# Two layers in one kernel: the second layer's first norm moved behind the first layer's last diagonal, and the norm's square moved from ACT to DVE

## The chip, the cores and the metric

The kernel runs on one core of a Trainium2 chip. Times are microseconds (us) on the device, from the program's first to its last instruction; the time of a kernel is the median of several runs. Engines are named as the profile names them: PE (TensorE matmuls), PEld (its weight loads), DVE (VectorE), ACT (ScalarE), POOL (GpSimd) and SP (SyncE, which issues most of the DMAs here). The profile is one execution, of which it shows every instruction.

## The reference

A batch of 16 images of 64 x 64 pixels and 128 channels goes through two layers, each behind a group norm and with its input added back:

```python
def _gn(v, G=32, eps=1e-5):
    g = v.reshape(B_, H_, W_, G, C_ // G)
    m = jnp.mean(g, axis=(1, 2, 4), keepdims=True)
    s = jnp.var(g, axis=(1, 2, 4), keepdims=True)
    return ((g - m) / jnp.sqrt(s + eps)).reshape(v.shape)
...
x = x + _L0_conv_ref(_gn(x), ...)   # a two-dimensional LSTM
x = x + _L1_conv_ref(_gn(x), ...)   # a Mamba block over the tokens, forwards and backwards
```

Layer 0 is a two-dimensional LSTM: the state of a pixel is made of those of the pixel above and the pixel to the left, by five gates (sigmoid or tanh of a product with the input and a product with the states). Layer 1 reads an image as a row of 4096 tokens: a projection and a causal convolution of four taps, SiLU, a softplus step size, then a scan with 16 states for each of 256 channels, weighted sums over the states, a gate, and a projection back. It does so in both directions, and the two are added. Everything is in float32. Each image's norm takes its mean and variance over all its pixels, so layer 1 can't normalise an image before layer 0 has written the whole of it.

## The kernel before

**Layer 0** (`layer0`) walks each image by diagonals, since the pixels of a diagonal don't need one another: 127 diagonals, of up to 64 pixels. The batch is cut into two halves of 8 images; the second half starts 13 diagonals behind the first, and the list `steps` takes turns between them: 254 steps. When the first half is done, diagonals 113 to 126 of the second half are left alone, steps 240 to 253. These are the lone diagonals. They have 14 pixels at first and 1 at last, for 8 images each, so 112 columns down to 8.

For each step `load` reads the next diagonal, turns it on PE (L855) and normalises it on DVE (L858, L863). `cell` multiplies with the gates' weights: ten matmuls, five on the input (L880), five on the states (L881). ACT takes the gates out of PSUM (L884), POOL makes one product (L892), DVE the others and the new cell state (L893 to L896), ACT its tanh (L897), DVE the new state h (L898), and the sum of two neighbours' states for the next diagonal (L874). `store` turns h back on PE (L907), adds the input on DVE (L913) and writes the result from ACT's queue (L915). h is what the next diagonal waits for.

Between its own instructions layer 0 does some of layer 1's work, so that layer 1 can begin at once. This work is the list `begin`: `weights`, then eight times `read` (one chunk of 512 tokens of image 0: a DMA at L1043, a turn on PE at L1051, a copy to the tile xT on ACT at L1056, statistics on DVE at L1061), then `first_normal` (image 0's norm), then eight times `normalise` (one chunk on ACT, L1073, scale and shift in place). The list `ready` holds the step from which each may be issued, and every step takes at most two. What is left when the steps are over is issued behind them. Each chunk's read becomes possible when its last rows have been stored; the last one at step 242. A scheduler then orders the instructions of layer 0 and of this list on each engine, by what they need from each other; the names say nothing of their places.

**The norm** (`group_norm`) is called twice by layer 0 (for 8 images each) and 16 times by layer 1 (one image each). It is a chain through three engines: group means by a matmul (L735), the difference dev on DVE (L737), its square sq (L739), two matmuls for the group's variance (L740, L741), the root on ACT (L743), for which ACT loads another table of functions, then the reciprocal and the shift on DVE (L745, L747).

**Layer 1** (`layer1`) works through 16 passes for each image, 8 chunks of 512 tokens forwards and 8 backwards. Its order isn't left to a scheduler: `order_of_issue` simulates the engines with costs and due times and writes every instruction's place out. In a pass PE makes the convolution (L1127, four matmuls for each half of the channels), ACT takes SiLU (L1137) and softplus (L1223), ACT the decays (da, L1248), DVE the scans (L1305), POOL the products ahead of 4 of the 16 states (L1256), of step size and input (dtx, L1229) and behind the scans of the other 12 (hc, L1328); PE sums these into PSUM (py, L1365) and makes the drive of the 12 from a matrix (hps, L1285). dtx is turned on PE (L1236) and copied by ACT (L1240). From image 1 on the norm of the next image stands in this same order: reading in the forward half of an image, norm at the beginning of its backward half, then the eight normalisations.

What both layers share is the rule of every engine: its instructions begin in the order in which they stand in its queue, and one that waits holds up those behind it.

Of the kernel before, what the change touches and what calls it, by code (L numbers as in the profile page):

```python
# [9 lines left out]
AF = mybir.ActivationFunctionType  # L10
# [15 lines left out]
NCH = L // T  # L26
# [670 lines left out]
def bc(ap, axis, n):  # L697

    ap = ap.unsqueeze(axis)
    shape = list(ap.shape)  # L700
    shape[axis] = n
    return ap.to_broadcast(shape)


@with_exitstack
def conv_preact_kernel(ctx: ExitStack, tc: tile.TileContext, a: dict):
    nc = tc.nc
    x, out = a["x"], a["out"]

    const = ctx.enter_context(tc.tile_pool(name="const", bufs=1))  # L710
    dram = ctx.enter_context(tc.tile_pool(name="dram", bufs=1, space=DRAM))
    x1 = dram.tile([B * L, C], F32, name="x1")


    ident = const.tile([P, P], F32, name="ident")
    make_identity(nc, ident)
    eps = const.tile([P, 1], F32, name="eps")
    nc.vector.memset(eps, GN_EPS)

    gavg = const.tile([P, P // GROUP, GROUP], F32, name="gavg")
    gsum = const.tile([P, P // GROUP], F32, name="gsum")
    nc.vector.tensor_reduce(
        gsum, ident.rearrange("p (g k) -> p g k", k=GROUP), mybir.AxisListType.X, ALU.add
    )
    nc.vector.tensor_scalar_mul(gavg, bc(gsum, 2, GROUP), 1.0 / GROUP)
    gavg = gavg.rearrange("p g k -> p (g k)")

    def group_norm(pool, mv, n, tag, bank):  # L730


        pm = bank(f"pm_{tag}", (P, 2, n))
        mean, pv = pm[:, 0, :], pm[:, 1, :]
        nc.tensor.matmul(mean, lhsT=gavg, rhs=mv[:, :, 0], start=True, stop=True)  # L735
        dev = pool.tile([P, n], F32, name=f"dev_{tag}", tag="gn_dev")
        nc.vector.tensor_sub(dev, mv[:, :, 0], mean)  # L737
        sq = pool.tile([P, n], F32, name=f"sq_{tag}", tag="gn_sq")
        nc.scalar.activation(sq, dev, AF.Square)  # L739
        nc.tensor.matmul(pv, lhsT=gavg, rhs=sq, start=True, stop=False)  # L740
        nc.tensor.matmul(pv, lhsT=gavg, rhs=mv[:, :, 1], start=False, stop=True)  # L741
        std = pool.tile([P, n], F32, name=f"std_{tag}", tag="gn_std")
        nc.scalar.activation(std, pv, AF.Sqrt, bias=eps)  # L743
        scale = pool.tile([P, n], F32, name=f"scale_{tag}", tag="gn_scale")
        nc.vector.reciprocal(scale, std)  # L745
        shift = pool.tile([P, n], F32, name=f"shift_{tag}", tag="gn_shift")
        nc.vector.scalar_tensor_tensor(shift, mean, -1.0, scale, ALU.mult, ALU.mult)  # L747
        return scale, shift


    diags = [
        {
            (kind, g): dram.tile([P, width], F32, name=f"{kind}_{i}_{g}")
            for kind, n, width in (("d", NA, WD), ("k", NG, T))
            for g in range(n)
        }
        for i in range(SETS)
    ]
    second = layer1(tc, a, const, ident, group_norm, x1, out, diags)
    layer0(tc, a, const, ident, group_norm, x, x1, [t for d in diags for t in d.values()], next(second))  # L760
    next(second, None)


def layer0(tc, a, const, ident, group_norm, x, x1, clear, begin):
# [4 lines left out]
    nc = tc.nc  # L769
    gates = ["f0", "f1", "i", "c", "o"]  # L770
    with ExitStack() as ctx:
# [148 lines left out]
        steps = []  # L920
        for t in range(ND + LATER):
            steps += [(t, 0)] * (t < ND) + [(t - LATER, 1)] * (t >= LATER)
        ready = [steps.index((WW - 1 + (c + 1) * T // WW - 1, 0)) + 3 for c in range(NCH)]
        ready = [81] + ready + ready[-1:] * (len(begin) - NCH - 1)
        FIRST = len(begin)
        before, now = None, load(*steps[0])
        for n in range(len(steps)):
# [573 lines left out]
```

## Time and profile before

| | |
|---|---|
| median of 3 runs | 12480.04 us (12465.78 to 12492.38) |
| the profiled execution's own time | 12473.08 us |
| its span, from first to last instruction | 12471.1 us |
| busy in the span | PE 11816.2, PEld 9141.1, DVE 11102.2, ACT 10217.3, POOL 10573.6 us |
| layer 0's last state h | 1512.31 us |
| layer 1's first convolution | 1513.46 us |
| POOL's first work in layer 1 (dtx) | 1539.02 us |
| norms of layer 1: image 0, 1, 2, then each about 682 us on | 1457, 1581, 2312 us |

How to read what follows: a row of the timeline has the start, the duration, engine, line, operation, what is written and what is read (buffer numbers left out), the shapes, and how many such instructions are merged. In brackets stands how long the engine had been idle before it, and whose end released it. "ACTq" is a DMA that ACT issued. In a table of windows, a row has the stretch, its length, the busy time of PE, PEld, DVE, ACT and POOL with the number of instructions, the granted clock of TensorE (1.00 is full), the share of the DMA engines and GB/s. Busy PE time is modelled and can be too full. A row of the page's groups has the number of instructions, their busy time and mean duration in ns, and the idle time before them with what ended it.

### The profile page before, as it was taken

The numbers are of one execution on the slowest core, as the hardware profiler recorded it, in microseconds if no ns is written. First come the engines' busy times: TensorE is split into PE (matmuls) and PEld (weight loads), VectorE is DVE, ScalarE is ACT, GpSimd is POOL, SyncE is SP. The second block draws the span as 40 slices with busy tenths as digits, with TensorE's granted clock in tenths as the row PEclk, the third lists the DMA queues.
The fourth block names the chain that finished last, engine by engine and source line by source line (L and its number), as shares of the span: only waits on it lengthen the run. The fifth ranks groups of instructions, "written<-read, shape, count | busy, mean of one in ns | idle before, by whom it ended". The sixth has DMA issues, their size and how long they took to land. (4 is left out here: it accounts for less than half of the span.)

```text
span 12471.1 us, 314271 instructions
## 1 busy us (share of the span) xinstructions
PE 11816.2 (95%) x123700; PEld 9141.1 (73%) x123700; DVE 11102.2 (89%) x11407; ACT 10217.3 (82%) x16448; POOL 10573.6 (85%) x4868
## 2 busy tenths in 40 slices
PE   9999989999999989899999999998999999999989
PEld 8656867777777767677777777776777777777777
DVE  7767589899999999999999999999999999999989
ACT  3444588888888888888888888888888888898888
POOL 0111199999999999999999999999999999999999
PEclk9999899999999999999999999999999999999999
DMA  4222255555555555555555555555555555555555
GB/s 156 56 56 56 56 152 167 159 166 161 163 167 157 169 158 164 158 170 158 165 163 163 160 164 167 155 167 158 167 158 169 160 162 164 163 165 162 163 154 149
DMA packets 2333045, 1885.43 MB, mean 151 GB/s; under 512 B 1549985, under 2 KB 1895601, under 8 KB 2331569
## 3 DMA queue, kind: packets, MB, share of 16 engines
q1 hardware_dynamic: 2253616, 1830.09, 51.0%
q10 hardware_dynamic: 77952, 35.24, 1.2%
q8 instruction: 977, 16.01, 0.5%
q14 instruction: 500, 4.09, 0.1%
HBM read 1698.25 MB, written 164.30 MB: 149 GB/s over the span
## 5 line engine op out<-in xcount | busy, mean ns | idle before, releaser
L1328 POOL TENSOR_TENSOR hc<-hst,cr 128x1024 f32<-128x1024 f32 x3072 | 7391.7, 2432 | 421.5 <-DVE hst L1305 303.8
L1305 DVE TENSOR_TENSOR_SCAN hst<-da,carry,hps 128x512 f32<-128x512 f32 x5376 | 6449.9, 1261 | 489.5 <-issue 188.4
L1248 ACT ACTIVATE da<-dt,A_log_sb 128x512 f32<-128x512 f32 x8192 | 5409.2, 711 | 805.3 <-DVE hst L1305 717.8
L1365 PE MATMUL py<-ident,hc 128*128 128x128 f32 x24576 | 3207.3, 277 | 31.8 <-POOL hc L1328 30.9
L1365 PEld LDWEIGHTS py<-ident,hc 128*128 128x128 f32 x24576 | 2812.4, 143 | 516.2 <-issue 346.6
L1256 POOL TENSOR_TENSOR group<-dtx,br 128x1024 f32<-128x1024 f32 x1024 | 2464.3, 2408 | 19.8 <-DMA br<-rows 10.4
L1305 DVE TENSOR_TENSOR_SCAN group<-da,carry,group 128x512 f32<-128x512 f32 x1792 | 2234.4, 1266 | 161.0 <-ACT da L1248 159.8
L1285 PEld LDWEIGHTS hps<-d,dtxt 32*128 32x128 f32 x49152 | 1545.4, 189 | 936.2 <-issue 583.1
L1285 PE MATMUL hps<-d,dtxt 32*128 32x128 f32 x49152 | 1835.7, 286 | 395.6 <-issue 237.0
L1127 PE MATMUL pp<-xT,wk 128*128 128x512 f32 x4096 | 1946.3, 595 | 0.9 <-DVE xl L913 0.5
L1345 ACT COPY ht<-ptg 128x512 f32<-128x512 f32 x2048 | 1125.7, 588 | 322.5 <-PE ptg L1337 290.3
L892 POOL TENSOR_TENSOR a_f<-a_f,c 128x16 f32<-128x16 f32 (+35 forms) x254 | 188.4, 742 | 1320.4 <-ACT a_f L884 1258.0
L1337 PE MATMUL ptg<-ident,group 128*128 128x128 f32 x8192 | 1193.6, 281 | 59.8 <-ACT ht L1345 33.8
L1337 PEld LDWEIGHTS ptg<-ident,group 128*128 128x128 f32 x8192 | 935.6, 143 | 283.4 <-issue 98.8
L1127 PEld LDWEIGHTS pp<-xT,wk 128*128 128x128 f32 x4096 | 696.9, 191 | 487.5 <-issue 481.0
L1305 DVE TENSOR_TENSOR_SCAN hst<-da,hps 128x512 f32<-128x512 f32 x768 | 875.3, 1200 | 77.1 <-issue 41.0
L1229 POOL TENSOR_TENSOR dtx<-dt,xc 128x512 f32<-128x512 f32 x512 | 651.7, 1288 | 124.8 <-ACT dt L1223 95.9
L1248 ACT ACT_TABLE_LOAD x527 | 676.1, 1283 | 9.3
L1352 PE MATMUL py<-ht,k 128*32 128x128 f32 x16384 | 568.0, 277 | 22.2 <-ACT ht L1345 22.2
L884 ACT ACTIVATE a_f<-pg_f,b_sb 128x16 f32<-128x16 f32 (+35 forms) x508 | 220.0, 473 | 419.1 <-DMA x<-xl 208.7
L1213 PE MATMUL pv<-dbl,dt_wT 128*128 128x256 f32 x2048 | 531.4, 392 | 0.0
L1352 PEld LDWEIGHTS py<-ht,k 128*32 128x32 f32 x16384 | 414.0, 110 | 112.0 <-issue 43.2
(113 smaller groups left out, 12180.2 us busy)
## 6 DMA issues: line engine op xcount, KB each, us to landing
cr<-rows SPq DMA_DIRECT2D x1536, 512.0 KB
d<-d SPq DMA_DIRECT2D x768, 448.0 KB
br<-rows SPq DMA_DIRECT2D x512, 512.0 KB
k<-k SPq DMA_DIRECT2D x256, 256.0 KB
yf<-y SPq DMA_DIRECT2D x128, 512.0 KB
yl<-yf SPq DMA_DIRECT2D x128, 512.0 KB
carry<-hst SPq DMA_DIRECT2D x3072, 1.0 KB
xs<-in_x_dram SPq DMA_DIRECT2D x64, 512.0 KB
```

Of the source, the lines that this page charges most:

```text
L1127: nc.tensor.matmul(self.ps["conv", h], lhsT=wk[:, k, h * P : (h + 1) * P], rhs=xT[self.b % 2][:, t0 : t0 + T], start=(k == 0), stop=(k == ...
L1213: nc.tensor.matmul(pv[:, q * TQ : (q + 1) * TQ], lhsT=dt_wT[:, q, h * P : (h + 1) * P], rhs=self.dbl, start=True, stop=True,)
L1229: nc.gpsimd.tensor_mul(self.dtx[h], self.dt[h], self.xc[h])
L1248: nc.scalar.activation(t, self.dt[h], AF.Exp, scale=amat[:, h, s : s + 1])
L1256: nc.gpsimd.tensor_mul(both[:, m : m + 2, :], bc(self.dtx[h], 1, 2), self.brow[q])
L1285: nc.tensor.matmul(part[:, j, :, :], lhsT=self.dtxt[h][rows, j, :], rhs=dg[rows, j + r, :, :], start=True, stop=True, skip_group_check=True,)
L1305: nc.vector.tensor_tensor_scan(t[:, self.rev], self.da.pop((s, h))[:, self.rev], dbx[:, self.rev], 0.0 if self.first else carry[:, self.d, ...
L1328: nc.gpsimd.tensor_mul(self.hc[g, h], self.hst[g, h].rearrange("p t m -> p m t"), self.crow[g])
L1337: nc.tensor.transpose(pt[:, k, :], self.group[g, h][:, t0 : t0 + TB, :].rearrange("p t s -> p (t s)"), ident,)
L1345: nc.scalar.copy(t, self.ps.pop(("turned", g, h, j)))
L1352: nc.tensor.matmul(self.py[h][q * TB : (q + 1) * TB, j * P : (j + 1) * P], lhsT=cd[:, GX * j + q, :], rhs=self.ht[g, h, j][:, q, :], start ...
L1365: nc.tensor.matmul(self.py[h][:, cols], **{"start": False, "stop": False, **how}, skip_group_check=True)
```

## The change

Two lines. The first moves the square in `group_norm` from ACT to DVE, for all 18 norms. The second changes the steps from which `first_normal` and the eight `normalise` of image 0 may be issued, from step 242 to a step that doesn't come: they are issued in the loop behind the last step. Before, `first_normal` went with step 242 (diagonal 115) and two normalisations with each of the steps 243 to 246. The weights and the eight reads keep their steps.

```diff
@@ group_norm
         sq = pool.tile([P, n], F32, name=f"sq_{tag}", tag="gn_sq")
-        nc.scalar.activation(sq, dev, AF.Square)
+        nc.vector.tensor_mul(sq, dev, dev)
         nc.tensor.matmul(pv, lhsT=gavg, rhs=sq, start=True, stop=False)
@@ layer0
         ready = [steps.index((WW - 1 + (c + 1) * T // WW - 1, 0)) + 3 for c in range(NCH)]
-        ready = [81] + ready + ready[-1:] * (len(begin) - NCH - 1)
+        ready = [81] + ready + [len(steps)] * (len(begin) - NCH - 1)
         FIRST = len(begin)
```

In the order of instructions that the changed kernel is built into, the aggregate of the statistics (L1084) still stands among the lone diagonals on DVE; L735 to L747 and the eight normalisations stand behind the last diagonal's instructions on PE, DVE and ACT. ACT keeps two table loads there of three: for the root, and for SiLU. In layer 1 every instruction keeps its place but the square; ACT's wait for dev, which the square had, now stands ahead of the table load.

## The prediction

> **What bounds the kernel now.** I read the page first, then the stretch in which layer 0 ends in a table of windows, then the timeline engine by engine around each place that the change touches.
>
> ```profile
> span 12471.1 us, 314271 instructions
> ...
> L1328 POOL TENSOR_TENSOR hc<-hst,cr 128x1024 f32<-128x1024 f32 x3072 | 7391.7, 2432 | 421.5 <-DVE hst L1305 303.8
> ```
>
> From about 1540 us on, layer 1 is bound by POOL in step with DVE: POOL is busy 9 tenths in every slice, and 303.8 of the 421.5 us that it idles before L1328 are waits for a scan of DVE. So a microsecond counts if it delays POOL's first work (the row at 1539.02 us, after 29.0 us of idling), or a scan that POOL waits for. The chain on the page covers the last 25 us alone and says nothing here.
>
> Of layer 0 only its end matters, the diagonals of the second half that run alone:
>
> ```profile
> 1447.50:1456.50 9.00, 6.05 (x51) 5.47 (x49) 5.18 (x20) 4.50 (x16) 0.80 (x2) 1.00 0.19 49
> 1471.00:1481.00 10.00, 10.00 (x46) 9.25 (x46) 3.89 (x20) 5.83 (x16) 0.65 (x2) 0.50 0.04 11
> 1490.00:1500.00 10.00, 10.00 (x49) 9.77 (x48) 3.02 (x19) 3.38 (x12) 0.52 (x2) 0.50 0.02 5
> 1500.00:1513.00 13.00, 11.58 (x56) 11.12 (x56) 3.62 (x22) 4.76 (x18) 0.66 (x3) 0.50 0.02 5
> ```
>
> The columns are the stretch, its length, busy time of PE, PEld, DVE, ACT, POOL, then the granted clock. At clock 1.00 PE has slack, and the state h (L898) comes 3.70 and 3.38 us apart (1449.45, 1453.15, 1456.53). From 1457.7 us the clock is 0.50, PE is full, and a diagonal takes 4.57 us ((1512.31 - 1484.87)/6), whatever its width.
>
> **Part 1: what leaves the lone diagonals.** ACT's rows show it:
>
> ```profile
> 1460.27 1.52 ACT L1073 ACTIVATE xT<-xT,shift_l,scale_l 128x512 f32<-128x512 f32 x2 [0.71 <-DVE shift_l L747]
> 1461.81 1.28 ACT L884 ACT_TABLE_LOAD   x1
> ```
>
> Between h of diagonal 115 (1456.53) and of 116 (1465.72) lie 9.19 us: the norm's chain, its table load, two normalisations and this reload. The next three diagonals carry two normalisations each and take 5.08, 4.99 and 4.90 us. All eleven take 1512.31 - 1456.53 = 55.8 us; at 4.57 each, 50.3. That is -5.5 us, the removed reload of 1.28 included.
>
> The clock may add to it. It fell at 1457.7 us, in a window in which PE stood idle for 1.94 us ahead of the norm. Without that pause some of the eleven keep the pace of 3.54: between none (0 us) and all (11 x 1.03 = -11.3). [...] I side with the rows: two diagonals at most (they still have 80 to 88 columns, the ones before had 96 to 112), -2.1 us. Part 1: -7.6 us.
>
> **Part 2: the handover, now bare.** In the built order, the mean's matmuls stand behind the last turn on PE, dev and sq behind the last L913 on DVE, load, root and eight normalisations behind the last store issue on ACT. No DMA is moved, SP's and POOL's queues keep their order, the layer's next reads are not touched.
>
> ```profile
> 1513.34 0.28 ACTq L915 DMA_DIRECT2D x<-xl  x1
> 1520.10 1.28 ACT L1137 ACT_TABLE_LOAD   x1 [7.83 <-PE pp L1127]
> ```
>
> Before, the first convolution starts at 1513.46. After, on the same clock of events: L735 ends about 1513.6 (a pair at half clock took 0.58), dev to 1513.76, sq to 1513.95 (POOL is idle there), L740 and L741 to 1515.0 (1.0 us at half clock, 1458.03 to 1459.04); the load, which now waits for dev, runs beside them to 1515.1. From root to normalisation it was 1459.30 to 1460.27, so the first normalisation starts at 1516.1 and takes 0.80. The convolution waits for that one alone and starts at 1516.95: +3.5 us. The other seven (7 x 0.75 us) end at 1522.2. What is late next is SiLU's load, which waits for four convolution matmuls, 6.64 us before (1513.46 to 1520.10), so at 1523.6: the seven hide with 1.4 us to spare. If the clock were warm there, the cover would be gone, and the load would start at 1522.2, still earlier. Part 2: +3.5 us, and it reaches POOL's first work in full.
>
> **Part 3: the square on DVE, in every image.** This is not a saving of 0.20 us on ACT. One norm of layer 1, DVE, ACT, POOL:
>
> ```profile
> 4361.30 0.16 DVE L737 TENSOR_TENSOR dev_l<-mv,pm_l 128x1 f32<-128x1 f32 x1 [1.67 <-PE pm_l L735]
> 4363.30 0.16 DVE L745 RECIPROCAL scale_l<-std_l 128x1 f32<-128x1 f32 x1 [1.84 <-ACT std_l L743]
> ```
> ```profile
> 4361.49 0.20 ACT L739 ACTIVATE sq_l<-dev_l 128x1 f32<-128x1 f32 x1 [1.77 <-DVE dev_l L737]
> 4361.71 1.28 ACT L743 ACT_TABLE_LOAD   x1
> 4363.00 0.26 ACT L743 ACTIVATE std_l<-pm_l,eps 128x1 f32<-128x1 f32 x1
> ```
> ```profile
> 4360.56 2.41 POOL L1328 TENSOR_TENSOR hc<-hst,cr 128x1024 f32<-128x1024 f32 x1
> 4366.19 2.40 POOL L1328 TENSOR_TENSOR hc<-hst,cr 128x1024 f32<-128x1024 f32 x1 [3.22 <-DVE hst L1305]
> ```
>
> DVE stands still for the root, and POOL then starves for 3.22 us: the root's start sets everything behind it, at 1.55 us after dev's end in each of 16 images. The load hides the square and the matmuls. Without any obstacle the root would come 0.22 us earlier. But sq would be the first DVE instruction of layer 1 with both inputs in SBUF (dev has one in PSUM, so has each scan), and POOL is inside an L1328. Layer 0 shows what such a pair does:
>
> ```profile
> 388.60 0.94 POOL L892 TENSOR_TENSOR a_f<-a_f,c 128x352 f32<-128x352 f32 x1 [4.67 <-ACT a_f L884]
> ```
> ```profile
> 389.00 0.92 DVE L893 TENSOR_TENSOR a_f<-a_f,c 128x352 f32<-128x352 f32 x1 [1.62 <-ACT a_f L884]
> 390.03 0.53 DVE L895 TENSOR_TENSOR a_f<-a_f,a_f 128x352 f32<-128x352 f32 x1
> ```
>
> L893 and L895 are alike, yet L893 takes 0.39 us more: POOL had 0.54 left when it started. Over L893's rows the extra is what POOL had left, less 0.13 to 0.15. [...]
>
> When dev ends, POOL's running L1328 has left, in the 14 images from the third on, 1.30, 1.67, 1.83, 1.52, 1.16, 0.97, 1.03, 0.12, 1.55, 1.75, 1.25, 1.94, 1.08 and 1.39 us. Then sq ends at left + 0.02 after dev's end, L741 0.66 later (0.24 to 0.90 in the rows), the root 0.05 after that: left + 0.73, and never before 1.33 (the load). Less 1.55, the sum is +7.5 us (image two, at 0.77 left, nothing). Behind the waiting L740 on PE stand L741, the turn of dtx (L1236) and 16 matmuls of py; the copy of that turn stands behind the root on ACT, ahead of the normalisations and of decays that DVE waits for: 0 to 0.4 us an image, I take 0.1: +1.5. [...] Layer 0's two norms (dev at 63.7 and 135.1 us) cost nothing: POOL is idle at both.
>
> **Sum.** -7.6 + 3.5 + 9 = +5 us on this execution's own 12473.08 us (span 12471.1). The median of the runs is 7 us above it; carried over, 12485 us.
>
> **Rivals.** (a) The clock stays warm through all lone diagonals: 9.2 us more from part 1 and 1.4 from part 2, 12474 us. For it: 10 us at 1.00 just before the norm. Against: narrower matmuls from then on. Chance 0.2. (b) The square doesn't wait for POOL: part 3 is -3.3, 12473 us. Against: L893. Chance 0.1. [...] Chance 0.07. (d) That the change doesn't do what it says is excluded for the order: the built order has it. The forecast's chance is 0.55; the rest, 0.08, is layer 1 starting at another phase of its transfers, either sign.
>
> **Numbers.** About 0.2%, 25 us, is what a measurement of this kernel can tell from no change; the three runs alone span 27 us. [...] Same 0.86, slower 0.10 ((c), and scatter on top of +5), faster 0.04. The range, 12462 to 12510, runs from (a) and (b) less 12 us to the forecast plus 12 us of scatter and half of (c).
>
> **What would show it.** h from diagonal 115 to 126 in 46 to 51 us, with the clock falling one to three diagonals later; the first convolution 3.5 us after the last L913; sq rows on DVE of 1 to 2 us, not 0.15; the root 2.0 us after dev. Sq rows of 0.15 us refute part 3; sq rows over 2.5 us mean (c); lone diagonals of 3.5 us to the end mean (a).

## The result and the profile after

The changed kernel takes 12491.34 us (median of 22 runs, 12462.89 to 12522.63), the kernel before 12473.43 us on the same chip (22 runs, 12456.31 to 12492.38). The ratio is 1.0015, with a 95% interval of [1.0008, 1.0021]: 18 us more, between 10 and 26. That is within the 0.2% that were called "same", and the time is 6 us above the forecast of 12485; the difference itself is not the +5 us of the sum.

The profiled execution took 12495.3 us. Its page:

```profile
span 12493.2 us, 314289 instructions
...
L1328 POOL TENSOR_TENSOR hc<-hst,cr 128x1024 f32<-128x1024 f32 x3072 | 7389.7, 2430 | 437.6 <-DVE hst L1305 323.7
```

POOL's work has kept its duration (7389.7 us, 7391.7 before); its idle time ahead of L1328 has grown from 421.5 to 437.6 us, and 19.9 us more of it than before are waits for a scan.

Layer 0's end, in the table of windows (columns as before):

```profile
1467.80:1480.00 12.20, 10.83 (x88) 9.79 (x87) 6.88 (x37) 5.68 (x23) 1.38 (x4) 1.00 0.09 22
1481.00:1491.00 10.00, 10.00 (x48) 9.66 (x47) 3.45 (x20) 3.70 (x13) 0.59 (x2) 0.50 0.05 13
1500.00:1510.00 10.00, 10.00 (x50) 9.93 (x50) 2.71 (x17) 3.20 (x12) 0.46 (x2) 0.50 0.01 4
```

The state h of diagonal 115 starts at 1467.76. The next four come 3.63, 3.31, 3.27 and 3.25 us apart at clock 1.00. At 1480.3 the clock falls to 0.50, and from there a diagonal takes 4.2 to 4.8 us as before.

The handover, on ACT and then on PE:

```profile
1514.22 1.28 ACT L743 ACT_TABLE_LOAD   x1 [1.43 <-DVE sq_l L739]
1515.52 0.26 ACT L743 ACTIVATE std_l<-pm_l,eps 128x1 f32<-128x1 f32 x1
1516.20 5.74 ACT L1073 ACTIVATE xT<-xT,shift_l,scale_l 128x512 f32<-128x512 f32 x8 [0.43 <-DVE shift_l L747]
1522.96 1.28 ACT L1137 ACT_TABLE_LOAD   x1 [1.02 <-issue]
```
```profile
1517.07 9.18 PE L1127 MATMUL pp<-xT,wk 128*128 128x512 f32 x16 [1.88 <-ACT xT L1073]
```

The convolution starts after the first of the eight normalisations; the last ends at 1521.94, ahead of SiLU's load at 1522.96.

A norm of layer 1, in image 2, on DVE, ACT, POOL and PE:

```profile
2313.93 0.15 DVE L737 TENSOR_TENSOR dev_l<-mv,pm_l 128x1 f32<-128x1 f32 x1 [1.76 <-PE pm_l L735]
2314.12 1.40 DVE L739 TENSOR_TENSOR sq_l<-dev_l 128x1 f32<-128x1 f32 x1
2316.51 0.16 DVE L745 RECIPROCAL scale_l<-std_l 128x1 f32<-128x1 f32 x1 [0.99 <-ACT std_l L743]
```
```profile
2314.16 1.28 ACT L743 ACT_TABLE_LOAD   x1 [1.84 <-DVE dev_l L737]
2316.22 0.26 ACT L743 ACTIVATE std_l<-pm_l,eps 128x1 f32<-128x1 f32 x1 [0.77 <-PE pm_l L741]
2316.87 0.59 ACT L1240 COPY dtxt<-ptx 128x512 f32<-128x512 f32 x1 [0.39 <-PE ptx L1236]
```
```profile
2310.72 4.78 POOL L1328 TENSOR_TENSOR hc<-hst,cr 128x1024 f32<-128x1024 f32 x2
2319.41 4.79 POOL L1328 TENSOR_TENSOR hc<-hst,cr 128x1024 f32<-128x1024 f32 x2 [3.91 <-DVE hst L1305]
```
```profile
2315.57 0.38 PE L740 MATMUL pm_l<-sq_l,gavg 128*128 128x1 f32 x2 [1.68 <-DVE sq_l L739]
```

POOL's running instructions (its first row) end at 2315.50, the square at 2315.52: it took 1.40 us and not 0.15. The root follows at 2316.22, after ACT had idled 0.77 us behind the table load. The copy of dtx's turn then waits 0.39 us more for PE, where it used to run right behind the root.

Where the time went, stage by stage, from the two profiled executions:

| stage | before | after | difference |
|---|---|---|---|
| start to diagonal 115 of the second half | 1456.53 us | 1467.76 us | +11.2 |
| lone diagonals, 115 to 126 | 55.8 | 45.1 | -10.7 |
| last state to first convolution | 1.15 | 4.25 | +3.1 |
| first convolution to POOL's first product | 25.6 | 24.8 | -0.8 |
| POOL's first product to the last instruction of an engine | 10928.9 | 10948.1 | +19.3 |

By POOL's pauses in a norm I mean, here and below, the time from dev's end to POOL's next product, and its next idle time, some 10 us later; the numbers are sums over the 14 norms of images 2 to 15. Of the last row, +13.7 us lie in these pauses (132.8 to 146.5 us). POOL's idle time around image 1's norm is 2.1 us longer (4.9 to 7.0), but in the profiles below it is anything from 5.3 to 7.0 us with the square on ACT too, so this need not be the square's. The row from the convolution to POOL's first product is 24.0 to 25.7 us in kernels without the move, so its -0.8 is scatter. The first row isn't in the forecast's sum at all.

### The profile page after: what moved, and what is told of

It reads as the page before. It is cut to its first block, busy times and chain, and to the rows that moved or that the text cites. A ratio compares the mean times of both kernels' runs of the same rounds, so it can differ in the third digit from the quotient of the medians.

```text
span 12493.2 us, 314289 instructions
## 1 busy us (share of the span) xinstructions
PE 11828.7 (95%) x123700; PEld 9153.0 (73%) x123700; DVE 11122.2 (89%) x11425; ACT 10210.3 (82%) x16429; POOL 10574.0 (85%) x4868
## 5 line engine op out<-in xcount | busy, mean ns | idle before, releaser
L1328 POOL TENSOR_TENSOR hc<-hst,cr 128x1024 f32<-128x1024 f32 x3072 | 7389.7, 2430 | 437.6 <-DVE hst L1305 323.7
L1256 POOL TENSOR_TENSOR group<-dtx,br 128x1024 f32<-128x1024 f32 x1024 | 2463.0, 2407 | 23.0 <-DMA br<-rows 10.8
```

Of the source, the lines that this page charges most:

```text
L1256: nc.gpsimd.tensor_mul(both[:, m : m + 2, :], bc(self.dtx[h], 1, 2), self.brow[q])
L1328: nc.gpsimd.tensor_mul(self.hc[g, h], self.hst[g, h].rearrange("p t m -> p m t"), self.crow[g])
```

## The experiments

**Theories.** Theory 1: the square on DVE waits for the rest of POOL's running instruction, so it costs in layer 1 what that rest decides. Theory 2: the square on DVE in layer 0's first norm brings the +11.2 us at the start. Theory 3: it is the move that costs, by what it does to layer 1's start, and that brings the 10 to 18 us. The rival to 1 is that layer 1's loss has another cause than this wait; the rival to 2 is chance. Twelve kernels ran in three sets of four, each on one chip beside the kernel before, which took 12570.48 us with the first set, 12551.09 with the second and 12569.45 with the third. None of them leaves out or changes a part of the computation; some add work whose result nobody uses.

**The move alone.** From the kernel before:

```diff
-        ready = [81] + ready + ready[-1:] * (len(begin) - NCH - 1)
+        ready = [81] + ready + [len(steps)] * (len(begin) - NCH - 1)
```

> The move alone, the square stays on ACT. [...] Theory 3 (the move costs, by what it does to layer 1's start): 10 to 18 us over before (1.001).

Measured: 12570.07 us, ratio 1.0001 [0.9993, 1.0009]. The lone diagonals take 44.1 us, with five of them at clock 1.00; the handover 4.42 us (+3.3). POOL's pauses in the norms are 133.1 us, as before. By stages that is -8 us, where theories 1 and 2 give -10.7 + 3.1 = -7.6; it lies at the edge of the interval (-9 to +11). So the move trades 3 us at the handover for diagonals that stay at clock 1.00, and theory 3 finds no loss in the stages; the gain is too small to be seen in the time.

**The square alone, in all 18 norms.**

```diff
-        nc.scalar.activation(sq, dev, AF.Square)
+        nc.vector.tensor_mul(sq, dev, dev)
```

> The square on DVE in all 18 norms, nothing moved. Theory 1: 15 us over before (1.0012), each square in layer 1 taking as long as POOL's running instruction still has (0.7 to 1.9 us), POOL's two pauses at each norm longer by 0.5 and 0.4 us. Theory 2: 10 us or so over before by h of the first diagonals alone, a later h at diagonal 113. Theory 3: no difference to before.

Measured: 12572.49 us, ratio 1.0003 [0.9994, 1.0012]. POOL's pauses are 134.3 us, only 1.2 more than with the square on ACT. One of its norms on DVE:

```profile
4400.02 0.66 DVE L739 TENSOR_TENSOR sq_l<-dev_l 128x1 f32<-128x1 f32 x1
4401.68 0.16 DVE L745 RECIPROCAL scale_l<-std_l 128x1 f32<-128x1 f32 x1 [0.99 <-ACT std_l L743]
```

POOL had 0.64 us left when this square began, and it took 0.66. On average over the 14 norms POOL had 0.44 us left when dev ended (nothing in three of them), where it was 1.33 in the profile before. So the square waits, but not for long enough to delay the root much. The expected +15 us weren't there because their size depends on a phase that differs between executions, and I had carried one chip's phase to another.

The norm of image 1 shows more, on DVE and then on POOL:

```profile
1583.06 4.62 DVE L739 TENSOR_TENSOR sq_l<-dev_l 128x1 f32<-128x1 f32 x1
```
```profile
1581.72 2.37 POOL L1256 TENSOR_TENSOR group<-dtx,br 128x1024 f32<-128x1024 f32 x1
1584.05 2.39 POOL L1328 TENSOR_TENSOR hc<-hst,cr 128x1024 f32<-128x1024 f32 x1
1586.41 1.25 POOL L1229 TENSOR_TENSOR dtx<-dt,xc 128x512 f32<-128x512 f32 x1
```

Here POOL goes on at once, and the square sits out three of its instructions: it ends at 1587.68, 0.02 us after the third. This is rival (c), in a norm: the square waits for the POOL instruction that follows as well, which in all 14 images would have been 34 us, 12519 us.

**Move, and the square on DVE in layer 0 alone.**

```diff
-        nc.scalar.activation(sq, dev, AF.Square)
+        if tag.startswith("l0"):
+            nc.vector.tensor_mul(sq, dev, dev)
+        else:
+            nc.scalar.activation(sq, dev, AF.Square)
```

> The move, with the square on DVE in layer 0's two norms only and on ACT in layer 1's. Theory 1: as the move alone, about 7 us under before (0.9994). Theory 2: 3 to 5 us over before (+10 at the start, -7 at the end of layer 0), with the clock at half rate beyond 100 us in the profile.

Measured: 12569.76 us, ratio 1.0000 [0.9991, 1.0009]; POOL's pauses are 133.1 us. The start shows clock 0.50 for 44.4 us. The lone diagonals take 52.5 us: here the clock fell with diagonal 115, at 1469.6, though no norm stood there.

```profile
1472.00:1482.00 10.00, 10.00 (x48) 9.60 (x47) 4.12 (x22) 3.58 (x11) 0.72 (x2) 0.50 0.06 14
```

With the clock at 0.50 through all eleven, the move saves 3.3 us and the handover takes 3.3 back.

**The changed kernel, with one input of layer 1's square in PSUM.**

```diff
-        nc.vector.tensor_sub(dev, mv[:, :, 0], mean)
+        if n == 1:
+            nc.vector.tensor_sub(dev, mean, mv[:, :, 0])
+        else:
+            nc.vector.tensor_sub(dev, mv[:, :, 0], mean)
...
-        nc.vector.tensor_mul(sq, dev, dev)
+        if n == 1:
+            nc.vector.scalar_tensor_tensor(sq, mean, mv[:, 0, 0:1], dev, ALU.subtract, ALU.mult)
+        else:
+            nc.vector.tensor_mul(sq, dev, dev)
```

> The changed kernel, but layer 1's square is one DVE instruction with one input in PSUM (group mean less own mean, times dev), so that it needs no second SBUF input; the difference dev is taken with the other sign. Theory 1: squares of 0.16 us, the root 1.33 us after dev, POOL's pauses 0.2 us shorter than before: 10 us under before by -7.6 of the two moved parts and -3 (0.9992), 25 us under the changed kernel. Theory 2: 10 us of the start remain, so about before (1.0000). If a wait of DVE has nothing to do with the second SBUF input: squares of 1 to 2 us as in the changed kernel, and its time.

Measured: 12563.81 us, ratio 0.9997 [0.9988, 1.0006]; POOL's pauses are 133.9 us. A norm on DVE, then on ACT:

```profile
4410.35 0.22 DVE L743 SCALAR_TENSOR_TENSOR sq_l<-pm_l,mv,dev_l 128x1 f32<-128x1 f32 x1
```
```profile
4410.65 1.28 ACT L749 ACT_TABLE_LOAD   x1 [2.10 <-DVE sq_l L743]
4411.94 0.26 ACT L749 ACTIVATE std_l<-pm_l,eps 128x1 f32<-128x1 f32 x1
```

The square takes 0.22 us while POOL runs (its L1334 lasted until 4410.95): no wait. The root comes 1.63 us after dev, later than 1.33, since the built order lets the table load wait for the square and not for dev. All 16 squares of layer 1 take 0.22 us. POOL's rest was again short in this execution (0.51 us), so its time can't tell the two squares apart; the rows can.

**The square on DVE in layer 1 alone, on the kernel before.** The edit is that of the third kernel with "l1" in the place of "l0", without the move.

> The kernel before with the square on DVE in layer 1's 16 norms alone; layer 0's two norms and the place of image 0's norm stay. Theory 1 (in layer 1 the square waits for the rest of POOL's running L1328): the square ends 0.02 us after that rest in each norm, and the root starts at rest + 0.72. If the rest is some 1.3 us on this chip, as on the chip of the first profiles, the pauses of POOL add up to 8 to 14 us more, and the time is 8 to 14 us longer; if it is 0.25 to 0.65 us, as in the four kernels before this, the time moves by less than 3 us. Theory 2 (the square of layer 0's first norm on DVE brings the long stretch of clock 0.50 at the start): here it is on ACT, so the stretch lasts under 15 us and the state of step 10 starts before 142 us. Rival to 2 (chance): anything from 7 to 65 us.

Measured: 12550.01 us, ratio 0.9999 [0.9991, 1.0008]. POOL had 0.73 us left on average; the pauses are 139.2 us, +6.1 over the 133.1 of ACT's square. One norm, on DVE and then on POOL:

```profile
9881.86 1.41 DVE L740 TENSOR_TENSOR sq_l<-dev_l 128x1 f32<-128x1 f32 x1
```
```profile
9878.48 4.78 POOL L1331 TENSOR_TENSOR hc<-hst,cr 128x1024 f32<-128x1024 f32 x2
```

In each of the 14 norms the square lasts as long as POOL's rest and 0.01 to 0.02 us more (0.79 and 0.81; 1.28 and 1.30; 1.40 and 1.41), or 0.16 where POOL stood still. Theory 1 holds in the rows; the time's interval holds +6 and holds nothing too. Theory 2 falls here: the square of layer 0 is on ACT, and the start has clock 0.50 for 61.4 us.

**The changed kernel again, without an edit.**

> The changed kernel as it is, again. Theory 2: clock 0.50 for over 20 us after the first norm, and the state of step 10 later than 142 us. Rival (chance): 7 to 65 us. Theory 1: root at the rest of POOL's instruction + 0.72 us; sum of POOL's pauses in 14 norms about 146 us if the rest is 1.3, about 134 if it is 0.3. The ratio to the kernel before: 1.0010 to 1.0020 where the rest is long, 0.9995 to 1.0005 where it is short.

Measured: 12552.83 us, ratio 0.9997 [0.9989, 1.0006]. POOL's rest is 0.81 us, the root comes 1.71 us after dev, the pauses are 138.7 us. The lone diagonals take 45.1 us and the handover 4.24, as in the first profile. The start has clock 0.50 for 13.7 us and step 10 at 136.3 us, with the square on DVE: theory 2 is wrong on this side as well. Its pauses are 8 us shorter than in its first profile, and on this chip the same kernel is not slower than the one before.

**The changed kernel, with layer 0's squares back on ACT.** The edit is again the choice by name.

> The changed kernel, with the square of layer 0's two norms back on ACT. Theory 2: it differs from the changed kernel by the start alone, clock 0.50 for under 15 us, the state of step 10 before 142 us, and so about 10 us faster than the changed kernel on the same chip. Rival (chance): the start is anything from 7 to 65 us of half clock, and the medians of the two agree within 5 us. Layer 1 as in the changed kernel: the square ends 0.02 us after the rest of POOL's instruction.

Measured: 12542.18 us, ratio 0.9991 [0.9983, 0.9999]. The start, as the table of windows has it:

```profile
62.00:100.00 38.00, 37.07 (x174) 35.74 (x175) 18.97 (x54) 7.76 (x22) 0.66 (x3) 0.50 0.51 169
100.00:132.00 32.00, 31.97 (x158) 30.02 (x157) 18.89 (x57) 6.48 (x23) 1.11 (x4) 0.53 0.51 175
```

and the same stretch of the changed kernel in its second profile:

```profile
62.00:100.00 38.00, 35.34 (x244) 32.50 (x245) 25.65 (x81) 10.00 (x32) 1.23 (x5) 0.82 0.64 213
100.00:132.00 32.00, 30.48 (x268) 28.55 (x266) 30.36 (x94) 8.78 (x34) 2.07 (x6) 1.00 0.62 205
```

PE is drawn busy for 37.07 of 38 and 31.97 of 32 us in the one and for 35.34 and 30.48 in the other, but issues 174 and 158 matmuls at clock 0.50 and 0.53, 244 and 268 at 0.82 and 1.00. The slow start is the one with the square on ACT. Over the 14 profiles, the longest stretch of 0.50 behind the first norm is 13.7, 6.8, 61.4, 68.3, 6.8, 23.9, 51.2, 64.9 and 13.7 us with the square on ACT there, and 64.9, 23.9, 44.4, 61.4 and 13.7 with it on DVE. Theory 2 had forecast a time some 10 us under that of the changed kernel on the same chip, chance one within 5 us. It is 10.7 us under (12542.18 and 12552.83), but resampling the 13 runs of each gives -21 to +2 for this difference, which decides nothing. By the profiles the rival, chance, stands; that the square adds a little to it is not excluded. Step 10 comes at 133 to 158 us and diagonal 115 behind it at 1451 to 1479, a spread of 28 us, where single runs of one kernel spread over 36 to 60.

**A version meant to beat both: the norm of layer 1 in six parts.** The kernel before, with each part placed by the planner on its engine, so that DVE need not stand still, and layer 1's square with its input in PSUM as above. The excerpt shows the planner's entries alone; their costs and the functions behind the names change with them.

```diff
-                    put("normal", (), "DVE", who=b + 1, key=("normal", b + 1), after=[...], takes=[m], uses=[m])
+                    put("normal", (), "DVE", who=b + 1, after=[...])
+                    put("normal_mean", (), "PE", who=b + 1, after=[get(("normal", b + 1))], takes=[m])
+                    put("normal_dev", (), "DVE", who=b + 1, after=[get(("normal_mean", b + 1))])
+                    put("normal_var", (), "PE", who=b + 1, after=[get(("normal_dev", b + 1))])
+                    put("normal_root", (), "ACT", who=b + 1, after=[get(("normal_var", b + 1))])
+                    put("normal_end", (), "DVE", who=b + 1, after=[get(("normal_root", b + 1))], uses=[m])
```

> The kernel before, with layer 1's norm cut into six parts that the planner places on their engines by themselves (aggregate, mean, difference and square from PSUM on DVE, variance, root, reciprocal and shift), so that DVE need not stand still for PE and for the root. If the stand of DVE is what a norm costs (theory: the root's start sets POOL's pause), the first pause of POOL, 4.7 us an image, goes nearly whole: 15 x 4 = 60 us less, 0.5%. If the second pause (4.7 us, behind the reload of the decays' table and the normalisations) goes as well, up to 130 us less, 1%. Rival: the norm only takes up slack that DVE or POOL has elsewhere in the pass, so that the pauses come back in another place: within 20 us of before. The planner's whole order changes behind the first norm, which may give 20 us of either sign by itself.

Measured: 12621.62 us, ratio 1.0052 [1.0039, 1.0065], slower by 65 us. The pauses did come back in another place, and longer. DVE, then POOL:

```profile
4403.43 1.28 DVE L1360 TENSOR_TENSOR_SCAN group<-da,carry,group 128x512 f32<-128x512 f32 x1 [0.46 <-ACT da L1303]
4405.87 0.16 DVE L780 RECIPROCAL scale_l<-std_l 128x1 f32<-128x1 f32 x1 [1.15 <-ACT std_l L777]
...
4409.56 1.28 DVE L1360 TENSOR_TENSOR_SCAN group<-da,carry,group 128x512 f32<-128x512 f32 x1 [3.34 <-ACT da L1303]
```
```profile
4413.42 2.43 POOL L1383 TENSOR_TENSOR hc<-hst,cr 128x1024 f32<-128x1024 f32 x1 [9.31 <-DVE hst L1360]
```

DVE now waits 3.34 us for a decay, which stands on ACT behind root, copy and the reload of its table; POOL's two pauses have become one of 9.31 us. In 14 norms they add up to 146.0 us, 13 more than with the norm in one piece. Where the other 50 us come from isn't shown; the planner's order of everything behind is new too.

**The wait by itself.** 512 more products of 128x1 elements on DVE, one behind a scan in each half of each pass. First with both inputs in SBUF, then with one in PSUM:

```diff
+                if s == NX + 1:
+                    junk = gp.tile([P, 1], F32, name=f"junk_{self.nm}_{h}", tag="junk")
+                    nc.vector.tensor_mul(junk, amat[:, h, 0:1], amat[:, h, 1:2])
```
```diff
+                    nc.vector.tensor_mul(junk, dbx[:, 0:1], amat[:, h, 1:2])
```

> The kernel before, with one more DVE instruction after one scan in each half of each pass of layer 1 (512 in all): a product of 128x1 elements, both inputs in SBUF, its result used by nothing. In the trace of before, POOL's running instruction has 0.88 us left on average when such a scan ends. [...]

> The same 512 products of 128x1 elements, after the same scans, but with one input in PSUM. [...] Rival (any small instruction behind a scan waits): rows of 0.9 us, as with two inputs in SBUF.

Measured, both in SBUF: 12661.4 us, ratio 1.0075 [1.0059, 1.009]. The group of the 512 (busy time, then mean ns):

```profile
L1315 DVE TENSOR_TENSOR junk<-A_log_sb 128x1 f32<-128x1 f32 x512 | 248.6, 485 | 0.0
```

One in PSUM: 12582.68 us, ratio 1.0011 [1.0002, 1.002].

```profile
L1315 DVE TENSOR_TENSOR junk<-hps,A_log_sb 128x1 f32<-128x1 f32 x512 | 68.2, 133 | 0.0
```

By theory 1 the rows with both inputs in SBUF were to last as long as POOL's rest, 0.9 us on average, and the time was to grow by 150 to 450 us; with one input in PSUM, rows of 0.15 to 0.25 us and 0 to 110 us. The rows do wait, and the size was put too large (92 us more, with one input in PSUM 13): behind these scans POOL had only 0.32 us left on average, not the 0.88 that was expected. With one input in PSUM no row is over 0.15 us. With both in SBUF the row is 0.13 us where POOL stands still; of the 241 that begin with more than 0.15 us of POOL's instruction left, 225 end within 0.05 us of its end (most 0.01 to 0.02 after it), and 16 do not. The tile amat has the name A_log_sb in the rows. One of those 16, on DVE and then on POOL:

```profile
1905.87 3.11 DVE L1315 TENSOR_TENSOR junk<-A_log_sb 128x1 f32<-128x1 f32 x1
```
```profile
1904.18 2.43 POOL L1256 TENSOR_TENSOR group<-dtx,br 128x1024 f32<-128x1024 f32 x1
1906.53 2.43 POOL L1331 TENSOR_TENSOR hc<-hst,cr 128x1024 f32<-128x1024 f32 x1
```

It sat out the rest of one POOL instruction and the whole of the next, until 1908.96; six of the 16 sat out two more. POOL goes on at once behind 239 of the 241, so mostly the product gets its turn even so. Of the ten that began behind an L1256 five lost it, of the 128 between two hc products one; why is open. The 180 us (248.6 - 68.2) that DVE is held longer turn into 79 us of time.

**The eight normalisations moved, the norm not.**

```diff
-        ready = [81] + ready + ready[-1:] * (len(begin) - NCH - 1)
+        ready = [81] + ready + ready[-1:] + [len(steps)] * (len(begin) - NCH - 2)
```

> The kernel before, with the eight normalisations of image 0 moved behind the last diagonal and its norm left at diagonal 115. Theory of the handover (the chain from mean to root is what costs, the first convolution waits for one normalisation of 0.8 us alone): from the last state to the first convolution 1.15 us as before or up to 1 us more, not 4.3. Lone diagonals: the gap behind diagonal 115 loses 1.5 us (two normalisations), the next three lose 0.4 each; 52 to 54 us in place of 55.8, the clock at 0.50 right behind 115 as before. In all -1 to -4 us, which the medians can't tell from nothing. Rival (the moved normalisations hold up ACT ahead of SiLU): first product of POOL later than 26.5 us behind the convolution, where it was 24.4 to 25.7.

Measured: 12561.7 us, ratio 0.9996 [0.9986, 1.0006]; lone diagonals 56.1 us, handover 1.15. The edit failed to do what it was for. With the scale known early, layer 0's scheduler put the normalisations back among the lone diagonals, between 1479.6 and 1500.2 us. It still shows something: the gap behind diagonal 115 is 9.19 us again, with no normalisation in it. So the two that stood there before cost nothing; the norm's chain and the clock do (5.8 us with the clock at 0.50 and no norm, in the third kernel).

**The input's matmuls issued twice in the lone diagonals.** On the kernel with the move alone:

```diff
+                if w and k > 113:
+                    nc.tensor.matmul(pgv, lhsT=w_sb[:, gi, :], rhs=xv, start=True, stop=True)
                 nc.tensor.matmul(pgv, lhsT=w_sb[:, gi, :], rhs=xv, start=True, stop=False)
```

> The kernel with the norm moved and its square on ACT, in which the five matmuls on the input are issued twice in the lone diagonals (the first result is overwritten by the second, so nothing changes in what is computed). They add about 0.6 us of PE's work to a diagonal at full clock, within the idle time it has there. Theory A (PE's idle time makes the clock fall): the clock stays at 1.00 for longer than the four diagonals behind 115 of the changed kernel, up to all eleven, which then take 38 to 42 us. Theory B (narrow matmuls with a weight load each don't count, however many): the clock falls at the same diagonals or sooner, a diagonal at 0.50 takes 5.5 to 6 us in place of 4.57, and the eleven take 52 to 62 us.

Measured: 12569.35 us, ratio 0.9995 [0.9987, 1.0004]; lone diagonals 55.3 us.

```profile
1458.00:1476.00 18.00, 18.00 (x157) 17.28 (x156) 8.44 (x45) 7.43 (x30) 1.68 (x5) 1.00 0.07 16
1478.00:1490.00 12.00, 12.00 (x58) 11.87 (x58) 2.57 (x16) 2.32 (x9) 0.27 (x1) 0.50 0.03 6
```

The clock stayed at 1.00 for 19.9 us behind diagonal 115. Of the other moved kernels, four kept it for 12.2 to 14.8 us and two not at all. Then a diagonal takes 6.3 to 7.0 us. In this one execution more work on PE held the clock for one or two diagonals more (theory A), but not to the end: PE was drawn busy for all 18.00 us from 1458 to 1476, and the clock still fell.

What separates the two clocks shows when the 14 profiles are taken together. The changes of the granted clock lie on a grid of 3.41 us: the 156 records of the profile before and the 142 of the one after keep to multiples of 3.4133 us within 0.6 ns. I counted for each such stretch the columns of all matmuls that begin in it (96 for a row of 128x96). From diagonal 113 to the last state, the clock stayed at 1.00 behind all 30 stretches with 1624 columns or more, it fell behind all 14 with 302 to 1552, and behind none of the 185 at 0.50, which had 1448 at most, did it come back. So in these 14 profiles the two sides part by the columns, and not by the share of time that PE is drawn busy: near diagonal 115 the changed kernel keeps 1.00 behind a stretch with 1.93 us busy and 1688 columns, the third kernel loses it behind one with 1.94 us and 1472, by where the grid lies. The norm's pause takes columns out (302 to 1018 in six of the seven kernels that have the norm at diagonal 115), narrower diagonals do it by themselves (1472 to 1552 in the seven moved ones), and at 0.50 no stretch held more than 1448. Here the extra matmuls kept the stretches at 1752 columns and more for longer, and the clock fell behind one of 1512. The count comes from finished profiles, and no run was made to test it. At layer 0's start the two sides overlap between 1416 and 1680 columns, and in layer 1, with many matmuls of 32 rows, the plain count doesn't separate them.

## Why the prediction was right or wrong

"Same" was right, and each mechanism was where it was said to be, but that the number came so near owes something to luck. The sum was +5 us, and the measured difference, +18 with an interval of 10 to 26, excludes it. The forecast of 12485 stood on a level of 12480 from three runs, 7 us above the median of 22. In the sum, terms of parts 1 and 3 were mis-sized in opposite directions, and one came that it didn't have.

**Part 1, the lone diagonals: -7.6 forecast, -10.7 measured, and -3.3 in two other profiles.** Both terms were wrong, and their errors cancel in part. The first, "at 4.57 each", took the pace of the narrow diagonals for the wide ones; with no normalisation between them the first takes 5.8 us at 0.50 and the next four 4.7 to 5.0. It is -3.3 and not -5.5, as the two moved kernels show whose clock fell at 115. The second, two diagonals that stay at full clock and -2.1, was the author's estimate, and no run shows it; it is -7.4 here. Four or five stay there in four of the moved kernels (45.1, 44.1, 45.1 and 45.3 us) and none in two (52.5 and 52.5). Rival (a) was half right: the clock stayed for four or five diagonals in four of them, but in no kernel to the end, and the argument against it, narrower matmuls, agrees with the count of columns (it fell behind 1472 to 1552).

**Part 2, the handover: +3.5 forecast, +3.1 measured** (1.15 to 4.25), and 3.1 to 3.3 in every kernel that has the move. From the start of the last L913 to the convolution it is 3.52 us, but it had been 0.43 before, so the 3.5 that was worked out is 0.4 too long: the mean's two matmuls begin within the last turn (1513.30 in the changed kernel) and end 0.91 us after h, where 1.29 had been taken. The seven other normalisations hid with 1.0 us to spare, where 1.4 had been worked out.

**Part 3, the square: +9 forecast (7.5 and 1.5), +13.7 measured in this execution.** That the square would wait for POOL's rest, the row of L893 carried to instructions of 2.4 us, is confirmed: it ends at the rest + 0.02 us. The root came at the rest + 0.72 in 12 of the 14 norms (forecast + 0.73), and POOL's first pause grew by 0.57 us an image, 8.0 in all, for the +7.5 of the forecast. What was mis-sized is the term behind PE's queue, "0 to 0.4 us an image, I take 0.1": the copy of dtx's turn is 0.4 us later (0.7 to 0.8 in four of the norms), the normalisations, the table's reload and the decays behind it too, and POOL's second pause grew by 0.40 in each of 14 images (+5.7 for +1.5). The upper end of the bracket was the right one, because that copy had stood right behind the root with no slack.

**The start: not in the sum, +11.2 in the profile.** By the profiles it is chance, and so belongs to no kernel. It made the profiled difference (22 us) larger than what the stages of the change explain.

**Open.** Parts 1 to 3 as measured give +6 us, +8 with image 1, which was put at nothing; the medians say +18, from 10 to 26. So 2 us at least are not assigned, and 10 by the medians; the starts of 22 runs need not have averaged out. Of the +19.3 behind POOL's first product, 3.5 lie outside the norms' pauses. And the sum is that of the first chip: where POOL's rest was 0.7 to 0.8 us, the pauses grew by 5 to 6 us, and at 0.44 by 1.2; there no kernel with the square or the move was measurably slower than before, the split norm aside.

**The rivals.** (b) is refuted by all 15 squares of the changed kernel that began while POOL ran. (c) happened to none of the 14 norms, in which POOL had nothing to go on with for the next 3.91 to 4.32 us. Where POOL went on at once, (c) is seen: 16 of 239 products waited for one or two POOL instructions more, and so did image 1's square in one of the five kernels that have it on DVE (4.62 us).

## What to carry to other kernels

Before a small DVE instruction with two SBUF inputs replaces one of another engine, look up what POOL still has to run at that moment, row by row: in the changed kernel's 14 norms the square took as long as that (0.74 to 1.90 us), and the mean rest was 0.44 to 1.35 us by the execution, so one chip's sum isn't the next one's. Look too whether POOL goes on at once behind that: here 16 of 239 such products waited for another instruction or two. Give it an input from PSUM, if one is at hand (0.22 us for the square, 0.13 for the products, with POOL running). Where a bracket has "what stands behind the waiting instruction" as one end, look whether that had any slack in the trace; without slack the end is the value.

## What the runs showed of the hardware

- A DVE product of 128x1 elements with both inputs in SBUF, begun while POOL ran, ended 0.01 to 0.02 us after POOL's running instruction in all 14 norms of the changed kernel (rows of 0.74 to 1.90 us); 512 products with one input in PSUM took 0.13 us on average, none over 0.15. Where POOL went on at once, 16 of 239 also waited for POOL's next one or two; the longest row is 4.62 us.
- PE at clock 0.50 was drawn full (10.00 of 10.00 us from 1481 to 1491 and from 1500 to 1510) and did not get its clock back: for 29 to 58 us on gate matmuls of 8 to 96 columns in the lone diagonals, and for up to 68 us on the wider ones of layer 0's start. Which execution has the long stretch at the start is not set by the kernel as far as 14 profiles show, and diagonal 115 comes at 1451 to 1479 us with it.
- In the lone diagonals of the 14 profiles, the clock of 1.00 stayed behind all 30 stretches of 3.41 us in which PE began 1624 columns or more; behind the 199 with 1552 or less 0.50 came or stayed. With half as many matmuls again, the clock stayed at 1.00 for 19.9 us in one execution.
- From layer 1's first convolution on, the profiled executions before and after began their instructions in the same order on each engine, the square left out: 116794 on PE, 8756 on DVE, 14878 on ACT; on POOL it is all 4868 of the program.
